# A graph network's first layer: own rows and input added by two accumulating DMAs into the sums' buffers, own rows stored already leaky, and a ninth mask made among the sums

## The chip, the core and the metric

The kernel runs on one core of a Trainium2 chip. The core has TensorE (PE, matmuls and transposes), VectorE (DVE), ScalarE (ACT), GpSimd (POOL) and SyncE (SP); each runs its own list of instructions in order, and waits on semaphores. DMAs are issued from the lists of SP, ScalarE and GpSimd. The metric is the device time of one execution in microseconds (us), lower is better.

## What is computed

A graph of 2708 nodes with 512 features, an adjacency matrix `adj` of integers (2708 x 2708, about 64 edges a row), and four layers, each followed by a residual and a layer norm. The change lies in layer 0; it also moves work of layer 1 that is prepared beside it:

```python
def L0(X, A, W_nb, b_nb, W_line, b_line):            # neighbours: the first 64 of each row
    Ab = A > 0
    keep = Ab & (cumsum(Ab, axis=1) <= 64)
    cnt = keep.sum(axis=1, keepdims=True)
    nb_mean = keep @ X / maximum(cnt, 1)
    xj = leaky_relu(nb_mean @ W_nb.T + b_nb)
    xi = leaky_relu(X @ W_line.T + b_line)            # the "own rows"
    return xi + where(cnt > 0, xj, 0)

def L1(x, adj, W_self, b_self, W_nb, b_nb, W_comb, b_comb):   # all neighbours
    mask = adj > 0
    agg = mask @ x / maximum(mask.sum(1), 1)
    return relu(concat([x @ W_self + b_self, agg @ W_nb + b_nb]) @ W_comb + b_comb)

x1 = layernorm(x + L0(x, ...))
x2 = layernorm(x1 + L1(x1, ...))
# layers 2 and 3: graph attention with 8 heads, then 8 heads and one head and a two-layer perceptron
```

## The kernel before

The 2708 rows are cut into `NT` = 22 tiles of 128 (the last, `LAST` = 21, has 20 rows). Products are taken before the sums: y = x W_nb is made once, and the neighbours' mean is a sum over y. y is kept as a high part `yH` and a low part `yL`, so each sum has two matmuls a neighbour tile. The change touches the first three of these stages.

**Layer 0's projections (0 to 193 us).** For each tile t: x is fetched and transposed by TensorE (L139, copied by L141), y = x W_nb (L300), split by ScalarE (L272) and VectorE (L277), own rows u = x W_line + b_line (bias added on VectorE, L452), stored to `r0_dram` by a GpSimd DMA (L453). Between these, masks are made, one for each tile of rows: loaded from `adj` with a cast to bf16 (L312, GpSimd's DMA), passed through a steep sigmoid that counts (`count`, L317, ScalarE), and in `place` a running sum over the row (a scan, L324) and a multiplication (L327) on VectorE mark the neighbours beyond the 64th. A finished mask must be transposed into `maskT`: either by TensorE, 22 transposes of 128 x 128 (`turn_here`, L336) and four signs on ScalarE (L340), or by one transposing DMA on SP (`turn`, L345) and four signs (L350). `HERE` = 14 masks are made in this stage; `now` spreads them over the tiles, and the even ones up to 10 are turned by DMA. Instructions on TensorE are held in the written order by `pe`, others by `issue_after`.

**Layer 0's sums (193 to 455 us).** The tiles of rows go in six blocks (`cuts`: five of four tiles, one of two). For each block and each neighbour tile j, ScalarE makes `kT` from `maskT` (L471), and TensorE adds into one PSUM buffer for each tile of the block (L639): eight matmuls a neighbour tile in the blocks of four. At the end ScalarE copies each sum to an SBUF buffer u, scaled by one over the count (L620). Beside the sums two generators are stepped by hand, and a scheduler puts their instructions into each engine's order:

- `both`, one step for each j: first `other_masks` (the remaining eight masks, 12 steps each: two half counts, four quarters of `place` of 677 columns, turn by DMA, signs at the next mask's steps), then `weights1` (W_nb and W_self of layer 1 multiplied into W_comb: rows fetched by SP, L205, transposed, L139, products, L300, a copy), then `vectors` (24 steps: a weight and an attention vector of layers 2 and 3 loaded by SP, L599 and L600, multiplied, L608, and reduced, L609).
- `todo`, two steps for each three j: `finish` of the block before. For each tile: bias (L530), leaky (L229), own rows fetched by SP (L205) into a `rows` buffer and made leaky (L229), x added onto them by an accumulating DMA (L534, GpSimd), combined with u (L536), layer norm (L121 to L128, its power on GpSimd, L126), x1 stored (L538), and its 32-bit words split into two halves of 16 bits (L149) and stored (L150) as `x1_words`.

**Layer 1's projections (455 to 612 us).** x1's transpose comes from `x1_words`: a transposing DMA on SP (L155) into a `rows` buffer (three of these), two tiles ahead, and a join on ScalarE (L161). Two products follow for each tile (L300): with the fused W_nb (split as before) and with the fused W_self (z, L667, stored by L669). The steps of `both` that are left (vectors) and of `todo` (the last block) come one a tile. Then layer 1's sums (612 to 830), and layers 2 and 3, which the change does not touch.

Of the kernel before, what the change touches and what calls it, by code (L numbers as in the profile page):

```python
# [10 lines left out]
F32 = mybir.dt.float32  # L11
# [9 lines left out]
P = 128  # L21
D = 512
# [10 lines left out]
def kernel(  # L33
# [18 lines left out]
    def rows(t):  # L52
        return min(P, N - t * P)
# [183 lines left out]
    with ExitStack() as phase:  # L237
# [65 lines left out]

        HERE = NT - 8
        cuts = [(b, min(b + 4, NT)) for b in range(0, NT, 4)]
        turns = range(NT)

# [47 lines left out]
        with ExitStack() as ph:  # L357
# [65 lines left out]
            for t in range(NT):  # L423
                n = rows(t)
                if t == END:
                    assert not due and turned >= HERE - 2
                    ends[:] = [end_tile(F32R) for _ in range(2)]
                    for y in (yH, yL):
                        nc.gpsimd.memset(y(LAST).bitcast(F32), 0.0)
                if t > 1:  # L430

                    lows[t] = keep_y(t, n, product(xTs(t, order=pe), n, wnT, 0, pe, sums() if t % 2 else None))
                xT = xTs(t)
                if t + 1 < NT:
                    xTs(t + 1, order=pe)
                while due and due[0][0] <= t:
                    signs_of(due.pop(0)[1], t)
                while turned < min(HERE, counted - (t + 2 < NT and not by_dma(turned))):
                    turn_next(turned)
                    turned += 1  # L440
                now = counted < min(HERE, -(-t * HERE // (NT - 4)))
                if now:
                    with tc.issue_after(stored[t - 1].ins) if t > 2 else nullcontext():
                        m = masks(counted)
                    places = st.tile([P, N // 2], BF16, name="places", bufs=1)
                    with tc.issue_after(highs[t].ins), tc.issue_after(copied[0].ins):
# [5 lines left out]
                low = nc.vector.tensor_add(u[:n], pm[:n], b_line[:n])  # L452
# [10 lines left out]
        with ExitStack() as ph:  # L463
# [10 lines left out]
            def other_masks():  # L474

                def room(i):
                    r = (ahead.tile([P, 2 * KD * (D + 2 * H)], BF16, name="w", tag="w", bufs=1) if i % 2 else
                         st.tile([P, 2 * KD * D], BF16, name="spare", tag="spare"))
                    m = r[:, :NT * P]
                    nc.gpsimd.memset(m[:, N if i < LAST else 0:], 0.0)  # L480
                    load_mask(i, m)
                    return m, r[:, NT * P:NT * P + N // 4 + 1]

                got, left = {HERE: room(HERE)}, iter(())
                into = weight2.rearrange("p k c -> p (k c)").bitcast(BF16)[:, :NT * P].rearrange("p (t n) -> p t n", n=P)
                for _ in range(5):
                    yield
                for i in range(HERE, NT):
                    if i + 1 < NT:
# [8 lines left out]
                    yield  # L498
                    for part in range(4):
                        place(i, m, places, part, 4)  # L500
                        if part == 3:
                            next(left, None)
                        yield
# [5 lines left out]
                    turn(i, m, into)  # L509
                    left = chain(signs(i, into), map(twins, turns[i:i + 1], [turns[i] + 1]))  # L510
                    yield
                    if i < LAST:
                        yield
                        yield
                signs_left.append(left)
                nc.vector.tensor_scalar(iso, cnts, 0.5, None, op0=OP.is_lt)
                nc.vector.tensor_scalar(rdeg, cnts, 1.0, None, op0=OP.max)
# [6 lines left out]
                nc.vector.reciprocal(one, one)  # L524

            def finish(ts_, us):
                r0s = early(1, len(ts_), lambda i: fetched(r0_dram, ts_[i], rows(ts_[i])))
                for i, t in enumerate(ts_):
                    n, u, r0 = rows(t), us[t], r0s(i)
                    nc.vector.tensor_add(u[:n], u[:n], b_nb[:n])  # L530
                    leaky(u[:n], u[:n])
                    with tc.issue_after(low.ins):
                        leaky(r0, r0)
                    nc.gpsimd.dma_start(r0, x[t * P:t * P + n, :], accum_op=OP.add)  # L534
                    yield
                    nc.vector.scalar_tensor_tensor(u[:n], u[:n], has[:n, t:t + 1], r0, op0=OP.mult, op1=OP.add)  # L536
                    layer_norm(sm, u[:n], n, u[:n])
                    nc.gpsimd.dma_start(x1_dram[t * P:t * P + n, :], u[:n])  # L538
                    yield
                    store_words(r0 if t % 2 or ts_ == range(*cuts[-1]) else words, x1_words, t, u)  # L540
                    yield


# [3 lines left out]
            bias1 = sm.tile([P, D], F32, name="bias1", bufs=1)  # L547

            def weights1():
                first, second = st.tile([P, KD, D], F32, name="spare", tag="spare"), weight2  # L550
                bcs = []
                order = [(w, m) for w in (l1_w_nb, l1_w_self) for m in range(KD)]
                load_weight(first, l1_w_comb[D:2 * D, :], nc.sync)
                nxt_rows = fetched(*order.pop(0), P)
                nc.sync.dma_start(bias1, bcast(l1_b_comb, D))
                for b_in in (l1_b_nb, l1_b_self):
                    bcs.append(sm.tile([P, KD], F32, name="bc"))
# [1 line left out]
                        nc.sync.dma_start(bcs[-1], b_in.rearrange("(k p) -> p k", p=P))  # L559
                yield  # L560
                for i, (bc, wc) in enumerate(zip(bcs, (first, second))):
                    dst = weight() if i == 0 else st.tile([P, KD, D], F32, name="spare", tag="spare")
# [59 lines left out]
            for i, b in enumerate(cuts):  # L622
                ts_ = range(*b)
                pa = {t: banks[t % 6]() for t in ts_}
                for j in range(NT):
                    if not kTs:
# [3 lines left out]
                            nxt, nxt_made = kept(b, following)  # L630
                        elif i + 1 < len(cuts):
                            nxt, nxt_made = kept(cuts[i + 1], 0)
                        with tc.issue_after(nxt_made.ins):
                            while copies:
                                copy_of(*copies.pop(0))
                    kT = kTs.pop(0)
                    for t in ts_:
                        for y in halves(j):
                            nc.tensor.matmul(pa[t], kT[:, (t - b[0]) * P:(t - b[0] + 1) * P], y(j),  # L639
                                             start=(j == 0 and y is yH), stop=(j == LAST))  # L640
                    if j % 3:
                        next(todo, None)
                    if len(ts_) > 2 or j % 2:
# [1020 lines left out]
```

## Time and profile before

| | |
|---|---|
| median of three runs | 2872.26 us (2871.07 to 2873.84) |
| the profiled execution | 2874.96 us |
| its span in the profile | 2873.2 us |
| granted TensorE clock, mean | 0.996 |
| layer 0's projections | 0 to 193 us |
| layer 0's sums | 193 to 455 us |
| layer 1's projections | 455 to 612 us |
| layer 1's sums | 612 to 830 us |

The profile has one execution on the core: a span from the first to the last instruction, busy time by engine, and groups of instructions by line of the kernel with what released them when they had waited. "PE acc L336 <- DVE u L452: 3.6" reads: a matmul of line 336 into the tile `acc` waited 3.6 us, and what ended the wait was VectorE's instruction of line 452 that writes `u`. Lines such as L300, L139, L205 and L229 are in helpers and stand for several places.

A few lines that give the durations of the work that the change moves (columns: line, engine, operation, output <- input, count, busy us, mean ns of one, idle time before and its releaser). First layer 0's projections:

```profile
L324 DVE TENSOR_TENSOR_SCAN places<-m,places,over 128x1354 bf16<-128x1354 bf16 x14 | 42.5, 3036 | 0.3
L327 DVE TENSOR_TENSOR m<-m,places 128x1354 bf16<-128x1354 bf16 x28 | 24.0, 859 | 0.4
L336 PE MATMUL acc<-identb,m 128*128 128x128 bf16 (+1 forms) x176 | 12.2, 220 | 3.6 <-DVE u L452 3.6
```

Then the sums and the start of layer 1's projections (193 to 480 us):

```profile
L530 DVE TENSOR_TENSOR u<-u,bias 128x512 f32<-128x512 f32 (+1 forms) x22 | 14.5, 672 | 5.4 <-ACT u L620 5.4
L229 DVE SCALAR_TENSOR_TENSOR rows<-rows 128x512 f32<-128x512 f32 x21 | 14.1, 684 | 29.0 <-DMA rows<-r_dram 29.0
L536 DVE SCALAR_TENSOR_TENSOR u<-u,has,rows 128x512 f32<-128x512 f32 x21 | 15.5, 745 | 21.1 <-DMA rows<-in_x_dram 21.1
```

### The profile page before, as it was taken

The numbers are of one execution on the slowest core, as the hardware profiler recorded it, in microseconds if no ns is written. First come the engines' busy times: TensorE is split into PE (matmuls) and PEld (weight loads), VectorE is DVE, ScalarE is ACT, GpSimd is POOL, SyncE is SP. The second block draws the span as 40 slices with busy tenths as digits, with TensorE's granted clock in tenths as the row PEclk, the third lists the DMA queues.
The fourth block names the chain that finished last, engine by engine and source line by source line (L and its number), as shares of the span: only waits on it lengthen the run. The fifth ranks groups of instructions, "written<-read, shape, count | busy, mean of one in ns | idle before, by whom it ended". The sixth has DMA issues, their size and how long they took to land. (4 is left out here: it accounts for less than half of the span.)

```text
span 2873.2 us, 35718 instructions
## 1 busy us (share of the span) xinstructions
PE 2801.1 (97%) x13910; PEld 1556.9 (54%) x13910; DVE 1992.8 (69%) x2372; ACT 1525.4 (53%) x1754; POOL 294.1 (10%) x457
## 2 busy tenths in 40 slices
PE   9999999999999999999999999999999999999998
PEld 5458764458886434444466433444385555555565
DVE  6856755643336999999978999999954435445342
ACT  4646642232336999999956999999950000000011
POOL 1112421111110000000021000000300010100001
PEclk9999999999999999999999999999999999999999
DMA  7745657533323011111152110111161000000000
GB/s 181 151 105 124 148 145 172 123 96 122 107 82 69 27 38 38 42 48 42 36 175 84 41 41 36 56 36 35 35 173 52 4 26 15 26 15 16 15 19 25
DMA packets 203654, 202.64 MB, mean 71 GB/s; under 512 B 126823, under 2 KB 151724, under 8 KB 203476
## 3 DMA queue, kind: packets, MB, share of 16 engines
q1 hardware_dynamic: 167592, 122.05, 16.2%
q0 software_dynamic: 24880, 74.01, 9.5%
q10 hardware_dynamic: 11004, 4.22, 0.6%
q8 instruction: 111, 1.82, 0.3%
q14 instruction: 67, 0.55, 0.1%
HBM read 137.90 MB, written 55.66 MB: 67 GB/s over the span
## 5 line engine op out<-in xcount | busy, mean ns | idle before, releaser
L894 DVE SCALAR_TENSOR_TENSOR e<-v_bc,ucol,maskT 128x1408 f32<-128x1408 f32 (+3 forms) x798 | 1133.0, 1483 | 315.5 <-PE pn L1295 307.3
L923 ACT ACTIVATE c<-e,bcol 128x1300 fp8e4<-128x1300 f32 (+2 forms) x688 | 956.7, 1412 | 61.7 <-DVE e L894 16.8
L1095 PE MATMUL po<-e,R 128*64 128x512 f32 (+3 forms) x4224 | 893.9, 549 | 25.8 <-DVE e L894 23.6
L1095 PEld LDWEIGHTS po<-e,R 128*64 128x64 f32 (+1 forms) x4224 | 333.7, 136 | 553.0 <-issue 390.0
L1295 PE MATMUL pn<-e,R 128*128 128x512 f32 (+1 forms) x1008 | 396.4, 557 | 0.8
L1295 PEld LDWEIGHTS pn<-e,R 128*128 128x128 f32 x1008 | 177.8, 190 | 195.5 <-issue 181.2
L1224 ACT ACTIVATE w<-pl,b 128x256 f32<-128x256 f32 (+1 forms) x88 | 40.9, 465 | 365.7 <-PE pl L1222 365.7
L126 POOL TENSOR_TENSOR ln_rs<-ln_rs,half 128x1 f32<-128x1 f32 (+1 forms) x88 | 56.7, 644 | 1321.6 <-DVE ln_rs L125 1300.4
L815 PE MATMUL pm<-w,xT 128*128 128x264 f32 (+1 forms) x704 | 164.1, 388 | 3.4 <-ACT xT L141 1.3
L686 PE MATMUL acc<-yH,mf 128*128 128x512 f32 x418 | 162.9, 390 | 0.0
L686 PE MATMUL acc<-yL,mf 128*128 128x512 f32 x418 | 162.8, 390 | 0.0
L1222 PE MATMUL pl<-lin 128*128 128x256 f32 (+1 forms) x704 | 152.9, 372 | 0.6 <-DVE lin L1124 0.6
L1247 PE MATMUL pl<-lin,w 128*128 128x512 f32 x336 | 150.8, 593 | 0.0
L1222 PEld LDWEIGHTS pl<-lin 128*128 128x128 f32 x704 | 129.5, 190 | 31.0 <-issue 15.8
L815 PEld LDWEIGHTS pm<-w,xT 128*128 128x128 f32 (+1 forms) x704 | 129.9, 190 | 28.9 <-ACT xT L141 3.5
L683 ACT CAST mf<-maskT 128x1024 fp32r<-128x1024 fp8e4 (+1 forms) x66 | 64.5, 978 | 142.9 <-PE acc L686 140.1
L995 PE MATMUL pd<-c,parts_c 128*12 128x384 fp8e4 (+2 forms) x2688 | 128.4, 307 | 0.0
L471 ACT ACTIVATE kT<-maskT 128x512 fp32r<-128x512 fp8e4 x121 | 75.9, 629 | 97.5 <-PE acc L639 80.3
L639 PE MATMUL acc<-yH,kT 128*128 128x512 f32 x304 | 123.0, 404 | 3.8 <-ACT kT L471 2.9
L300 PE MATMUL acc<-w,xT 128*128 128x512 f32 (+1 forms) x256 | 117.3, 602 | 5.1 <-ACT xT L161 2.7
L639 PE MATMUL acc<-yL,kT 128*128 128x512 f32 x304 | 119.9, 394 | 0.0
L1313 ACT COPY lin<-pn 128x512 f32<-128x512 f32 (+1 forms) x12 | 5.8, 538 | 204.6 <-PE pn L1295 204.6
(291 smaller groups left out, 3007.9 us busy)
## 6 DMA issues: line engine op xcount, KB each, us to landing
v_bc<-v_dram SPq DMA_DIRECT2D x16, 704.0 KB
x_dram<-u POOLq DMA_DIRECT2D x42, 256.0 KB, 2.4
v_bc<-v_dram SPq DMA_DIRECT2D x16, 650.0 KB
m<-in_adj_dram POOLq DMA_DIRECT2D x14, 677.0 KB, 7.1
rows<-in_x_dram SPq DMA_DIRECT2D x21, 256.0 KB
r_dram<-u POOLq DMA_DIRECT2D x21, 256.0 KB, 3.5
rows<-r_dram SPq DMA_DIRECT2D x21, 256.0 KB
rows<-in_x_dram POOLq DMA_DIRECT2D x21, 256.0 KB, 4.8
```

The costliest lines, as they stand in the source:

```text
L300: order(nc.tensor.matmul(pm[:m], xT[:, k, :m], w[:, k, :], start=(k == 0), stop=(k == KD - 1)))
L471: made = nc.scalar.activation(kT, maskT[:, j:j + g, b[0] * P:b[0] * P + w], AF.Relu, scale=-1.0)
L639: nc.tensor.matmul(pa[t], kT[:, (t - b[0]) * P:(t - b[0] + 1) * P], y(j), start=(j == 0 and y is yH), stop=(j == LAST))
L686: nc.tensor.matmul(pa, mf[:, j - g0, :], y(j), start=(j == 0 and y is yH), stop=(j == LAST))
L815: nc.tensor.matmul(pm[a][:m, :D // 2 + heads], xT[:, k, :m], w[:, k, a, :D // 2 + heads], start=(k == 0), stop=(k == KD - 1))
L894: self.made = nc.vector.scalar_tensor_tensor(e[:, :w], v[:, :w], ucol[:, j, h:h + 1], maskT[:, j, c0:c0 + w], op0=OP.max, op1=OP.mult)
L923: nc.scalar.activation(c[:, :w], e[:, :w], AF.Sigmoid, bias=bcol[:, j, h:h + 1], scale=STEP, saturate=False)
L995: pe(nc.tensor.matmul(p[32 * g:32 * g + 12, :c1 - c0], parts_c[:, j, h, :], c[:, c0:c1], start=(i == 0 and h == hs[0]), stop=(i == NT - 1 ...
L1095: pe(nc.tensor.matmul(po[i][HO * k:HO * k + HO, :c1 - c0], R2[at, j, h * HO:(h + 1) * HO], e[at, a:a + c1 - c0], start=(i_ == 0), stop=(i_ ...
L1222: nc.tensor.matmul(pl[:, :w], self.lin1[:, k, f * P:(f + 1) * P], h[:, k, :w], start=(k == 0), stop=(k == KD - 1))
L1247: nc.tensor.matmul(pl[:n], gT[:, f, (t - t0) * P:(t - t0) * P + n], self.lin2[:, f, :], start=(f == 0), stop=(f == KF - 1))
L1295: nc.tensor.matmul(pn[k][:, :w], R2[at, j, k * P:(k + 1) * P], e[at, :w], start=(j == 0), stop=(j == NT - 1))
```

## The change

- **Own rows are stored leaky.** In layer 0's projections a leaky on VectorE follows the bias add, before the store to `r0_dram`.
- **Two accumulating DMAs.** `finish` puts the bias on in one instruction (b_nb where the row has a neighbour, plus u), makes u leaky, and adds x and then the own rows from `r0_dram` into u by two accumulating DMAs on GpSimd's queue. This first step is taken for all tiles of the block, then layer norm, store and words for each. The fetch of own rows, their leaky and the combining instruction are gone; words of odd tiles and of the last block's tiles go into new `rows` buffers.
- **Nine masks among the sums.** `HERE` is 13, so eight masks become nine there, with ten steps for each instead of twelve, and a first wait of three steps instead of five.
- **Weight rows one ahead.** `weights1` fetches its rows one step before they are used, and its loading step is taken within the last mask's steps; the two large buffers `w` and `spare` swap roles.
- **Copies of the last two sums of a block** are made one a neighbour tile, at j = 1 and 2 of the next block, instead of both at once.

```diff
-        HERE = NT - 8
+        HERE = NT - 9
...
-                low = nc.vector.tensor_add(u[:n], pm[:n], b_line[:n])
+                nc.vector.tensor_add(u[:n], pm[:n], b_line[:n])
+                low = leaky(u[:n], u[:n])
                 stored[t] = nc.gpsimd.dma_start(r0_dram[t * P:t * P + n, :], u[:n])
...
-                for _ in range(5):
+                for _ in range(3):
                     yield
...
                         place(i, m, places, part, 4)
+                        if part == 0 and i == LAST:
+                            next(made_weights)
...
                     left = chain(signs(i, into), map(twins, turns[i:i + 1], [turns[i] + 1]))
                     yield
-                    if i < LAST:
-                        yield
-                        yield
...
             def finish(ts_, us):
-                r0s = early(1, len(ts_), lambda i: fetched(r0_dram, ts_[i], rows(ts_[i])))
-                for i, t in enumerate(ts_):
-                    n, u, r0 = rows(t), us[t], r0s(i)
-                    nc.vector.tensor_add(u[:n], u[:n], b_nb[:n])
+                for t in ts_:
+                    n, u = rows(t), us[t]
+                    nc.vector.scalar_tensor_tensor(u[:n], b_nb[:n], has[:n, t:t + 1], u[:n], op0=OP.mult, op1=OP.add)
                     leaky(u[:n], u[:n])
-                    with tc.issue_after(low.ins):
-                        leaky(r0, r0)
-                    nc.gpsimd.dma_start(r0, x[t * P:t * P + n, :], accum_op=OP.add)
+                    for src in (x, r0_dram):
+                        nc.gpsimd.dma_start(u[:n], src[t * P:t * P + n, :], accum_op=OP.add)
                     yield
-                    nc.vector.scalar_tensor_tensor(u[:n], u[:n], has[:n, t:t + 1], r0, op0=OP.mult, op1=OP.add)
+                for t in ts_:
+                    n, u = rows(t), us[t]
                     layer_norm(sm, u[:n], n, u[:n])
                     nc.gpsimd.dma_start(x1_dram[t * P:t * P + n, :], u[:n])
                     yield
-                    store_words(r0 if t % 2 or ts_ == range(*cuts[-1]) else words, x1_words, t, u)
+                    if t < LAST:
+                        even = t % 2 == 0 and t < cuts[-1][0]
+                        store_words(words if even else ahead.tile([P, D], F32, name="rows", bufs=3), x1_words, t, u)
                     yield
...
-                order = [(w, m) for w in (l1_w_nb, l1_w_self) for m in range(KD)]
+                w_rows = early(1, 2 * KD, lambda i: fetched((l1_w_nb, l1_w_self)[i // KD], i % KD, P))
                 load_weight(first, l1_w_comb[D:2 * D, :], nc.sync)
-                nxt_rows = fetched(*order.pop(0), P)
+                w_rows(0)
...
-                        xT = transposed(ahead, ps_tr, nxt_rows, P, "xT")
-                        nxt_rows = fetched(*order.pop(0), P) if order else None
+                        xT = transposed(ahead, ps_tr, w_rows(i * KD + m), P, "xT")
...
-            todo, both = iter(()), chain(other_masks(), weights1(), vectors())
+            made_weights = weights1()
+            todo, both = iter(()), chain(other_masks(), made_weights, vectors())
...
-                        with tc.issue_after(nxt_made.ins):
-                            while copies:
-                                copy_of(*copies.pop(0))
...
+                    if copies and j:
+                        with tc.issue_after(nxt_made.ins):
+                            copy_of(*copies.pop(0))
```

More of the change, by code (lines that the diff above doesn't have):

```diff
@@ L476, in room @@
                 def room(i):
-                    r = (ahead.tile([P, 2 * KD * (D + 2 * H)], BF16, name="w", tag="w", bufs=1) if i % 2 else
+                    r = (ahead.tile([P, 2 * KD * (D + 2 * H)], BF16, name="w", tag="w", bufs=1) if (i - HERE) % 2 else
                          st.tile([P, 2 * KD * D], BF16, name="spare", tag="spare"))
@@ L549, in weights1 @@
             def weights1():
-                first, second = st.tile([P, KD, D], F32, name="spare", tag="spare"), weight2
+                first, second = weight(), weight2
                 bcs = []
-                order = [(w, m) for w in (l1_w_nb, l1_w_self) for m in range(KD)]
+                w_rows = early(1, 2 * KD, lambda i: fetched((l1_w_nb, l1_w_self)[i // KD], i % KD, P))
                 load_weight(first, l1_w_comb[D:2 * D, :], nc.sync)
-                nxt_rows = fetched(*order.pop(0), P)
+                w_rows(0)
                 nc.sync.dma_start(bias1, bcast(l1_b_comb, D))
@@ L561, in weights1 @@
                 for i, (bc, wc) in enumerate(zip(bcs, (first, second))):
-                    dst = weight() if i == 0 else st.tile([P, KD, D], F32, name="spare", tag="spare")
+                    dst = weight() if i else st.tile([P, KD, D], F32, name="spare", tag="spare")
                     made1.append(dst)
```

## The prediction

> **What bounds the kernel now.** I read the busy totals first, then the same totals stage by stage (the stretches are layer 0's projections to 193 us, its sums to 455, layer 1's projections to 612, its sums to 830, the rest), then what ended TensorE's idle time in each.
>
> ```profile
> PE 2801.1 (97%) x13910; PEld 1556.9 (54%) x13910; DVE 1992.8 (69%) x2372; ACT 1525.4 (53%) x1754; POOL 294.1 (10%) x457
> ```
> ```profile
> 0.00:193.00 193.00, 185.31 (x666) 93.32 (x666) 141.02 (x128) 100.50 (x133) 32.30 (x64) 0.99 0.70 153
> 193.00:455.00 262.00, 252.69 (x1043) 194.35 (x1043) 164.94 (x278) 137.54 (x222) 75.51 (x102) 0.99 0.62 139
> 455.00:612.00 157.00, 150.89 (x359) 64.65 (x357) 93.77 (x124) 37.41 (x47) 19.06 (x31) 0.99 0.50 118
> ```
> The columns are stretch, its length, then busy time of PE, PE loads, VectorE, ScalarE, GpSimd. TensorE is busy 96% of each stretch, so VectorE, ScalarE and DMA work that goes away is worth nothing by itself: VectorE has 52, 97 and 63 us to spare. Only TensorE's own instructions and its waits can move the end. The diff touches nothing behind 612 us. The waits of TensorE, by stretch:
>
> ```profile
> PE acc L336 <- DVE u L452: 3.6, 1, 3.6
> PE acc L370 <- DVE ones L69: 1.1, 1, 1.1
> PE acc L300 <- DVE weight L178: 0.9, 1, 0.9
> PE acc L300 <- ACT maskT L340: 0.7, 1, 0.7
> ```
> ```profile
> PE ps_tr L139 <- DMA rows<-in_L_gnn_W_nb_dram: 4.3, 1, 4.3
> PE acc L639 <- ACT kT L471: 2.9, 1, 2.9
> PE acc L639 <- ACT u L620: 0.8, 1, 0.8
> PE ps_tr L139 <- DMA rows<-in_L_gnn_W_self_dram: 0.7, 1, 0.7
> ```
> ```profile
> PE acc L300 <- ACT xT L161: 2.7, 1, 2.7
> PE acc L300 <- DVE ln_rs L125: 1.6, 1, 1.6
> ```
> (waiting line, releaser, us in total, times, longest). Some 17 us in all, and the change can only win there and in removed matmuls. A long wait costs more than itself:
>
> ```profile
> 85.83 1.06 PE L336 MATMUL acc<-identb,m 128*128 128x128 bf16 x16
> 90.45 0.59 PE L336 MATMUL acc<-identb,m 128*128 128x128 bf16 x6 [3.55 <-DVE u L452]
> 90.97 5.40 PE L300 MATMUL pm<-weight,xT 128*128 128x512 f32 x8
> ```
> The eight products after the 3.55 us wait take 5.40 us where eight take 3.60 elsewhere in this stretch: 1.80 us more. The trace shows the same after the waits of 2.70, 2.93 and 4.34 us, not after 1.58.
>
> **A, layer 0's projections.** A turn by TensorE (22 transposes, L336) goes, since 13 masks instead of 14 are made here: 0.91 us for 16 plus 0.52 for 6 in the timeline, -1.43. The 3.55 us wait goes: it is mask 5's turn at tile 9, which needs a PSUM buffer freed by tile 8's bias add, and that add stood behind a 2.97 us scan on VectorE (86.84 to 89.73). In the new order this turn comes at tile 10, a tile after that add. -3.55 and -1.80. The 0.70 wait for L340, at another turn whose place moves, -0.70. Added: 21 leaky (L229, 0.68 us, one each 0.60) on VectorE, which also sheds two scans of 1354 (2 x 3.0) and two multiplications (2 x 0.86). VectorE's cycle of a tile with a mask grows from 8.87 to 9.47 us, so mask 1's second multiplication, which ends at 46.7 as TensorE gets to its turn, ends two leakys later: +1.3. At tile 15's turn the third group of transposes needs tile 14's add, again behind a scan: about 1.65 of the 3 us of that scan are left, +1.65. **A = -4.5** (-8 if neither new wait comes; up to +4 if two waits of 3.5 with their slow matmuls do: 13 x 7.7 + 18 x 2.03 = 137 us of VectorE stand in 141 us of TensorE there).
>
> **B, the sums.** Own rows come as an accumulating DMA into u (L532) instead of a fetch on SP, a leaky, an accumulate and an add: VectorE sheds 0.68 + 0.68 us for each of 22 tiles, worth nothing alone. A second accumulate waits for the first to land; one lands 4.73 us after its issue (median of L534, 3.09 to 9.15), so a tile is 2 x 4.7 us late where it was one. All four tiles are started before the first layer norm, and 14 calls of the block's list stand for 12 steps, so the block's 40 us hide it. Gone: the 2.93 us wait for kT at 319.22, behind a u copy (L620) that waited 1.86 us for the store of the old u, with 1.6 us of slow matmuls, and the 0.79 at 313.08 (copies now come one per neighbour tile, a block later than the store); the 4.34 at 385.03 with 1.3 slow and the 0.69 at 439.73 (weight rows are fetched one ahead). Sum -11.65. Added: ScalarE does two copies (0.69), two half counts (1.41) and kT (0.63) at a block's start, +1.3. On SP the transpose of mask 20 now stands behind a W_nb row fetch, whose buffer is free only when words of tile 11 have landed, some 38.4 us into block 3; behind the transpose (5.5 us at the shortest here) stand the signs of mask 20 on ScalarE's queue, then kT: a gap of 2.1 and 0.4 slow. The second W_comb load stands behind a W_self row fetch that waits for tile 13's words: +0.7. Signs of mask 21 +0.3. A ninth mask here takes the steps that each of the others gave up (10 instead of 12), 2.1 us of scan and multiplication a step. **B = -6.9** (-12 with no new wait, +4 if the queue's wait is as long as the transposed mask's own landing, 7.3, and comes twice).
>
> On this rests a rule that speaks against the change. The Trainium skill, "DMA: Bandwidth & Descriptors", section "Rules for kernel authors", says that an accumulating DMA beside another access of the same bytes can lose data and must wait for the earlier one's semaphore. The instruction order has just that wait on GpSimd's queue ahead of every second accumulate. By the rule alone the end of each block's rows is a landing later, which is what part C prices.
>
> **C, from the last block of sums to layer 1's projections.** Before, the first two transposed tiles xT (L161) were made at 441.9 and 446.2, before the sums ended at 455. In the new order SP issues the transposes of x_words behind the attention vectors' loads (L600): the load for step 7 waits for VectorE's reduce (L609) of step 5, which stands on VectorE behind tile 19's layer norm, which waits for its second accumulate. Worked from the start of the last block: tile 16's x is issued at 1.8, lands 6.5, its own rows 11.2; the others alternate on GpSimd's queue, tile 17's at 8.3, tile 18's at 12.1, then a store of x1, tile 19's at 14.9, landing 19.6. Twelve VectorE instructions follow to L609 of step 5 (eight at 0.6, four small, one wait of 0.75 for GpSimd's power): 25.5. The transpose lands some 3.7 later (3.5 to 4 here), 29.3, and ScalarE's join takes 1.17: 30.5. The sums end at 86 x 0.2285 = 19.7. TensorE waits 10.8, and 2.1 of slow matmuls: +12.9. The waits that stood here go: 1.58, 2.70 with 1.9 slow, two of 0.8 together: -7.0. **C = +5.9**. If VectorE's order didn't bind, tile 15's words and two u copies would still leave 5: -2; with none, -7; what it takes upwards is rival 3.
>
> The rule beside these rows is in the Trainium skill, "TensorE: Matmul & The Clock Gate", Part 1: half clock after about one idle window of 3.4 us, full clock after about as long busy. This trace has slow matmuls after a wait of 2.70 already, so the row decides; by the rule, as an estimate from that page, a wait of 10.8 costs at most half of 3.4, 1.7, in slow matmuls instead of 2.1, and the sum would be 0.4 lower.
>
> **Sum.** -4.5 - 6.9 + 5.9 = -5.5. The profiled execution took 2874.96 (span 2873.2), so 2869.5; the median of the three runs, 2872.26, is 2.7 below the profiled one, so **2866.7**.
>
> **Rivals.** (1) The wait in C is small: VectorE does its ready reduces without waiting for tile 19. For: VectorE is busy 60% there. Against: its instructions run in program order. C = -2 to -5, sum -13 to -16: about 2857. (2) New waits in B eat its gain: SP's queue carries mask transposes behind fetches that wait for words; in the trace SP already waits 83.7 us for words to land. B = -2 to +1, sum -1 to +2: about 2873. (3) Slower: in layer 1's projections SP's queue alternates transpose and vector load, and a load waits for VectorE's pair of the step two before. If nothing of that overlaps, a tile's round is a vector step (2.7 to 3.4), the transpose's landing (3.5 to 4) and the join (1.17): 7.4 to 8.6, against TensorE's 2 x 3.44 = 6.9 for a tile. Over some ten tiles that is +5 to +17 on top of C. It decides from 1.2 us a tile on, where the sum -5.5 + 12 passes +5.7; from there to 1.7 it is +6 to +11: about 2880. For: every transpose but two has a load ahead of it. Against: three buffers of rows let transposes run ahead, and the sum of parts that overlap is less. (4) The diff doesn't do what it says: no sign; the order has 22 more accumulates and 22 fewer fetches of own rows.
>
> **Chances.** Forecast (-2 to -10, 2862 to 2870) 0.42; (1) 0.22; (2) 0.20; (3) 0.16. A difference of 0.2%, 5.7 us, is about what a measurement of this kernel can tell from no change: half of the forecast's own case lies below -5.7 (0.22) and half above. Faster 0.22 + 0.22 = 0.44; same 0.20 + 0.20 = 0.40; slower 0.16. The range leaves out the best fifth of (1) and the upper two thirds of (3), together some 0.15: 2856 to 2879.
>
> **What would show it.** A: no wait of L336 for L452 at tile 9, 154 transposes L336 instead of 176, waits of 1 to 2 us at tiles 4 and 15. B: no wait for W_nb rows, none for the u copy, one of about 2 us for kT early in block 4. C: a wait of 7 to 12 us of the first L300 of layer 1 for xT, ended by a transpose. Wrong if that wait is under 5 (then rival 1), if waits for kT in the sums come to over 8 (rival 2), or if more than two waits over 2 us stand behind the first in layer 1's projections (rival 3).

## The result and the profile after

The changed kernel takes 2918.25 us (median of six, 2909.96 to 2922.66) where the kernel before takes 2875.25 beside it (2871.07 to 2878.51): ratio 1.0146, 95% interval 1.0127 to 1.0165. The profiled execution took 2910.97, span 2909.1; before it was 2874.96 and 2873.2. So the kernel is slower, by 36 us in the profiles and 43 in the medians, where -5.5 was forecast. The profiled execution is one of the two fastest of the six, so the last 7 us of the medians stand in no trace; what follows explains the 36.

The totals of the page, then the first three of the four stretches (length, then busy time of PE, PE loads, VectorE, ScalarE and GpSimd, granted clock, DMA share, GB/s), cut at the changed kernel's own borders: first matmul of the sums, last one, first matmul of layer 1's sums. In the kernel before these lie at 188.8, 455.0 and 613.5; the prediction's view of it was cut at 193, 455 and 612.

```profile
PE 2802.9 (96%) x13888; PEld 1556.4 (54%) x13888; DVE 1984.4 (68%) x2355; ACT 1525.8 (52%) x1756; POOL 306.5 (11%) x480
```
```profile
0.00:193.30 193.30, 180.54 (x634) 90.54 (x634) 145.47 (x144) 94.08 (x125) 30.26 (x58) 0.98 0.63 144
193.30:473.70 280.40, 259.60 (x1053) 196.81 (x1052) 150.75 (x240) 141.78 (x229) 82.74 (x120) 0.97 0.67 131
473.70:645.10 171.40, 151.47 (x361) 65.54 (x360) 96.77 (x131) 42.18 (x51) 26.34 (x42) 0.95 0.53 127
```

TensorE does the same work (2802.9 against 2801.1 us, 22 transposes fewer), so the 36 us are nearly all waits, and matmuls at the lower clock after them. Measured between the same events, before and after: projections 188.8 and 193.3, sums 266.2 and 280.4, layer 1's projections 158.5 and 171.4, the rest 2259.7 and 2264.0. That is +4.5, +14.2, +12.9 and +4.3. VectorE, which the change relieves, has lost 8 us of work, and the kernel is slower all the same. TensorE's waits in the three stretches, in this order:

```profile
PE acc L300 <- ACT maskT L340: 5.3, 1, 5.3
PE acc L336 <- DVE u L452: 3.1, 1, 3.1
```
```profile
PE pm L637 <- ACT kT L472: 11.5, 3, 7.9
PE ps_tr L300 <- issue: 3.5, 1, 3.5
PE pm L637 <- ACT u L621: 3.1, 1, 3.1
PE acc L637 <- ACT kT L472: 2.3, 3, 1.0
```
```profile
PE acc L300 <- ACT xT L161: 17.7, 1, 17.7
```

The waits that the change was expected to end are gone: none for W_nb rows, none at 90 us, none behind a u copy at 319. Others, longer, stand in their place.

**The 17.7 us wait** is the forecast one of part C. Three views of it, by time: GpSimd's DMA issues, VectorE, and SP's queue, from the last block of sums on (block start 453.8, its sums' end 473.7).

```profile
468.77 0.84 POOL L532 DMA_DIRECT2D u<-r_dram  x1 [3.91 <-DMA u<-in_x_dram]
...
472.11 0.89 POOL L532 DMA_DIRECT2D u<-r_dram  x1
```
```profile
478.07 0.69 DVE L121 BATCH_NORM_STATS2 ln_st<-u 128x6 f32<-128x512 f32 x1 [3.47 <-DMA u<-r_dram]
...
483.53 0.68 DVE L609 TENSOR_REDUCE wa<-weight 128x8 f32<-128x512 f32 x1
```
```profile
474.47 10.13 SPq L600 DMA_DIRECT2D weight<-in_L_gnn_W_dram  x3
484.65 3.87 SPq L155 DMA_TRANSPOSE rows<-x_words  x2
```

Own rows of tile 19 are issued at 472.11 and land at 478.0; the reduce behind that layer norm ends at 484.2; only then SP's third load of the three in the view goes, and behind it, at 484.65, the first transpose of x_words. ScalarE's join waits for it until 490.36, and TensorE's first product of layer 1 starts at 491.57. The accumulates' medians from issue to landing, in us (last column), where the kernel before had 4.73:

```profile
u<-in_x_dram POOLq DMA_DIRECT2D x21, 256.0 KB, 6.4
u<-r_dram POOLq DMA_DIRECT2D x21, 256.0 KB, 5.0
```

**The 7.9 us wait** in the sums, at 380.73, is the one that was forecast with 2.1. SP again, then ScalarE:

```profile
362.64 10.43 SPq L205 DMA_DIRECT2D rows<-in_L_gnn_W_nb_dram  x2
373.23 3.89 SPq L345 DMA_TRANSPOSE weight<-w  x1
```
```profile
379.10 1.06 ACT L350 ACTIVATE maskT<-weight 128x1024 fp8e4<-128x1024 bf16 x1 [8.56 <-DMA weight<-w]
380.06 0.61 ACT L472 ACTIVATE kT<-maskT 128x512 fp32r<-128x512 fp8e4 x1
```

The second fetch of a weight row stands 10 us for words of tile 11 to land; the transpose of mask 20 is behind it; its signs head ScalarE's queue for 8.56 us, and kT, for which TensorE waits, stands behind the signs.

**Three more waits in the sums.** The next longest for kT, 3.4 us at 273.32, has the same form, but no fetch of a weight row is ahead of its transpose. The transpose itself is slow, and so is an accumulate issued beside it, which landed at 268.49. GpSimd, SP and ScalarE:

```profile
256.71 0.85 POOL L532 DMA_DIRECT2D u<-r_dram  x1 [0.46 <-DMA u<-in_x_dram]
```
```profile
256.73 7.04 SPq L345 DMA_TRANSPOSE weight<-spare  x1
```
```profile
271.69 1.06 ACT L350 ACTIVATE maskT<-weight 128x1024 fp8e4<-128x1024 bf16 x1 [4.64 <-DMA weight<-spare]
```

The wait of 3.1 us for a u copy, at 285.7, stands behind a half count on ScalarE that waited 2.2 us for its mask's load. The one of 3.5 us, for which the profile names no releaser, is put down here to W_comb's second load: it ends at 426.25, and VectorE's first instruction on the same tile, at 426.18, was released by that load:

```profile
L575 DVE SCALAR_TENSOR_TENSOR u<-weight,bc,u 128x512 f32<-128x512 f32 x4 | 3.0, 752 | 11.9 <-DMA weight<-in_L_gnn_W_comb_dram 11.8
```

**The 5.3 us wait** in the projections, at 104.08, was not forecast:

```profile
91.92 0.54 POOL L454 DMA_DIRECT2D r_dram<-u  x1 [5.06 <-DVE u L229]
...
92.58 0.73 POOL L312 DMA_DIRECT2D m<-in_adj_dram  x1
```
```profile
100.47 2.55 ACT L317 ACTIVATE m<-m,gate 128x2708 bf16<-128x2708 bf16 x1 [6.01 <-DMA m<-in_adj_dram]
...
103.02 2.64 ACT L340 ACTIVATE maskT<-acc 128x1024 fp8e4<-128x1024 bf16 x4
```

The store of own rows waits on GpSimd's queue for the new leaky; the next mask's load is behind the store and lands 7.8 us later; the count waits for it; and the signs of the turn before, which free TensorE's PSUM buffers, are behind the count.

### The profile page after: what moved, and what is told of

Read it like the earlier page. It is cut to its first block, busy times and chain, and to the rows that moved or that the text cites. A ratio compares the mean times of both kernels' runs of the same rounds, so it can differ in the third digit from the quotient of the medians.

```text
span 2909.1 us, 35610 instructions
## 1 busy us (share of the span) xinstructions
PE 2802.9 (96%) x13888; PEld 1556.4 (54%) x13888; DVE 1984.4 (68%) x2355; ACT 1525.8 (52%) x1756; POOL 306.5 (11%) x480
## 3 DMA queue, kind: packets, MB, share of 16 engines
q0 software_dynamic: 27984, 79.55, 10.6%
```

## The experiments

Ratios are to the kernel before, run on the same chip. The stage times are of each profiled execution, between the events named above; "start wait" is TensorE's longest wait ahead of layer 1's first products. Kernels whose code is the same in a stage differ there by up to 4 us (seven kernels have the changed kernel's first stage: 191.5 to 195.4).

| kernel | ratio (95%) | projections | sums | layer 1's projections | start wait |
|---|---|---|---|---|---|
| before | 1 | 188.8 | 266.2 | 158.5 | none |
| changed | 1.0146 (1.0127 to 1.0165) | 193.3 | 280.4 | 171.4 | 17.7 |
| b_finish | 1.0061 (1.0044 to 1.0078) | 190.3 | 276.5 | 156.9 | none |
| b_nine | 0.9991 (0.9981 to 1.0000) | 185.6 | 269.0 | 155.5 | none |
| b_rows | 0.9995 (0.9986 to 1.0005) | 189.4 | 264.3 | 159.2 | none |
| b_copies | 1.0010 (1.0000 to 1.0020) | 190.3 | 268.4 | 158.2 | none |
| a_old_finish | 1.0018 (1.0009 to 1.0028) | 185.3 | 272.3 | 158.3 | 3.2 |
| b_finish_nine | 1.0091 (1.0074 to 1.0108) | 195.2 | 276.1 | 166.7 | 13.7 |
| a_vec_late | 1.0120 (1.0103 to 1.0137) | 191.5 | 277.1 | 171.0 | 17.0 |
| a_step_late | 1.0116 (1.0099 to 1.0133) | 195.4 | 277.1 | 168.0 | 14.4 |
| a_no_x | 1.0008 (0.9998 to 1.0017) | 191.8 | 259.5 | 161.3 | 7.6 |
| a_no_leaky | 1.0138 (1.0121 to 1.0155) | 186.4 | 283.2 | 171.5 | 17.2 |
| a_front | 1.0082 (1.0065 to 1.0098) | 191.5 | 276.8 | 157.5 | none |
| a_sum_store | 1.0041 (1.0026 to 1.0056) | 212.1 | 259.5 | 160.4 | 5.9 |
| a_per_tile | 1.0116 (1.0100 to 1.0133) | 194.7 | 282.4 | 172.4 | 13.2 |
| c_gp_add | 1.0073 (1.0051 to 1.0095) | 216.1 | 256.7 | 151.2 | none |
| c_nine_fetch | 1.0055 (1.0037 to 1.0073) | 221.2 | 260.2 | 151.2 | none |
| c_eight_fetch | 1.0032 (1.0019 to 1.0045) | 215.7 | 255.1 | 150.5 | none |
| d_eight_early_x | 0.9999 (0.9991 to 1.0008) | 202.4 | 255.2 | 151.9 | none |
| d_nine_early_x | 0.9992 (0.9983 to 1.0001) | 199.1 | 258.6 | 151.2 | none |

### The parts alone

Each is a part of the change's own diff on the kernel before. **b_finish** has the leaky at the store and the new `finish`:

```diff
+                low = leaky(u[:n], u[:n])
...
+                    for src in (x, r0_dram):
+                        nc.gpsimd.dma_start(u[:n], src[t * P:t * P + n, :], accum_op=OP.add)
```

> The kernel before with the new finish alone: own rows stored leaky, two accumulating DMAs into u, words of odd tiles in new buffers; masks, weight rows, copies as before. Queue theory (the loss of 36 us is short instructions standing in an in-order queue behind DMA landings that the change made later, above all SP's transposes of x_words behind vector loads that start earlier): the vectors start where they did, so only a landing of 5 us comes on top at the last block: +3 to +10 us. DMA theory (42 accumulates of 256 KB beside mask loads and transposes make every DMA slower): +15 to +25 us, most of it in the sums. Mask theory (the ninth mask overfills the sums): within 4 us of before.

+0.61%, some 17 us: the DMA theory's range, and over half of it (10.3 us) in the sums. Layer 1's start has no long wait. In the projections, with 14 masks as before, the leaky shows 1.5 us, less than kernels with the same code differ by.

**b_nine** has the ninth mask, the shorter steps, and `w` and `spare` swapped:

```diff
+        HERE = NT - 9
...
-                    if i < LAST:
-                        yield
-                        yield
```

> The kernel before with nine masks among the sums in ten steps each (13 in the projections), w and spare swapped; finish, weight rows and copies as before. Queue theory: the vectors start at the last block's start, as in the changed kernel, and the transposes of x_words stand behind their loads, with one accumulate less ahead: a wait of 5 to 10 us at layer 1's start, the sums some 3 us worse by the crowding of the masks, 1.4 us won by one turn less: +5 to +15 us. DMA theory: 0 to +5. Mask theory: +20 to +30, most of it in the sums.

-0.09%. The queue theory's +5 to +15 and the mask theory's +20 are both out; the DMA theory's 0 to +5 is nearest. The vectors start as early here as in the changed kernel, 4 to 5 us ahead of the last block, and with one accumulate less there is no long wait behind them.

**b_rows** and **b_copies**:

```diff
+                w_rows = early(1, 2 * KD, lambda i: fetched((l1_w_nb, l1_w_self)[i // KD], i % KD, P))
```
```diff
+                    if copies and j:
+                        with tc.issue_after(nxt_made.ins):
+                            copy_of(*copies.pop(0))
```

> The kernel before with the weight rows fetched one ahead, nothing else. All theories: the 4.34 us wait for W_nb rows with 1.3 us of slow matmuls and the 0.69 for W_self rows go: -4 to -6. If the early fetch stands behind words that have not landed, it only moves: 0.

> The kernel before with the copies of a block's last two sums made one a neighbour tile at j = 1 and 2, nothing else. All theories: the 2.93 us wait for kT at 319 us with 1.6 us of slow matmuls and part of the 0.79 us go: -3 to -5.

Neither is a gain that the measurement tells from none. In b_rows the wait for W_nb rows is 3.04 us instead of 4.34, and the one for W_self rows 0.54 instead of 0.69. In b_copies the stall behind the u copy is ended (the copy waits 0.18 us for its store instead of 1.86), but another comes, of 4.11 at 328.5: kT behind the signs of a mask, which wait 5.38 us for its transpose. Part B had counted both stalls as gone.

**a_old_finish**: the changed kernel with the `finish` and the store of before, so b_finish's lines taken back:

```diff
-                low = leaky(u[:n], u[:n])
...
+                    nc.gpsimd.dma_start(r0, x[t * P:t * P + n, :], accum_op=OP.add)
```

> The changed kernel with the finish of before (own rows fetched, made leaky there, one accumulate) and own rows stored as before; nine masks, weight rows and copies as changed. By parts alone (+17, -3, -0.5, +3) the finish is the only dear part, but the parts come to +17 and the whole to +42. Theory 1, interaction: the finish is dear because the nine masks put vectors, counts and transposes into the steps where its landings fall, so without it the rest is near before: -4 to +3. Theory 2, the nine masks are dear with the other small parts: +15 to +25.

+0.18%, some 5 us (interval 2.6 to 8.0): without the new finish the change is near before. Theory 2 falls; theory 1 is near, with its -4 to +3 a little low.

**b_finish_nine**: the two diffs of b_finish and b_nine together.

> The kernel before with the new finish and the nine masks; weight rows and copies as before. Theory 1: the interaction is between these two, +35 to +42, with the long wait for x_words at layer 1's start and the long waits in the projections. Theory 2: they add, +14.

+0.91%, where the two alone add to +0.52%. The interaction is there, though not all of the +1.46%: by the stages alone one would add up to 187.1, 279.3 and 153.9; together they have 195.2, 276.1 and 166.7, so 8 us in the projections and 13 at layer 1's start come from the two meeting. The changed kernel adds weight rows one ahead and the copies, which were worth nothing alone, and with them come 4.3 us more in the sums and 4.7 more at layer 1's start of the profiles, and 0.55% in the ratios; which of the two does it was not tried.

### The queue in front of layer 1, and the mask transpose

**a_vec_late** and **a_step_late**:

```diff
             def vectors():
+                for _ in range(11):
+                    yield
```
```diff
-                        if part == 0 and i == LAST:
-                            next(made_weights)
```

> The changed kernel, with eleven empty steps before the attention vectors, so that their loads come behind the first transposes of x_words on SP and no vector stands in VectorE's queue in the last block. Queue theory: the 17.7 us wait at layer 1's start falls to about the chain of landings itself (tile 16's words need the copy, two landings, layer norm, a store and a transpose), to 4 to 8 us: -10 to -14. Rival: the wait is set by the accumulates and the u copies, and stays over 14: -4 to 0.

> The changed kernel without the early loading step of the weights, so that SP's transpose of mask 20 no longer stands behind the fetch of a weight row that waits for words of tile 11. Queue theory: the 7.88 us wait for kT with some 1.2 us of slow matmuls goes, and a wait of up to 6 for W_comb or weight rows takes its place: -3 to -9. Rival: the signs wait for the transpose's own landing, and the wait stays: within 3 us of the changed kernel.

Neither did what it was made for. The waits stay (17.0, and 7.5 for kT), but in a_vec_late's trace several vector loads still stand ahead of the first transpose on SP, and in a_step_late's the weight rows' fetch still stands ahead of mask 20's transpose: the scheduler orders SP's queue, and the edits did not change this. They do not refute the queue. But a_vec_late shows that it is not the whole wait: its first transpose is issued 5 us after the sums' end instead of 11, and ScalarE's join waits for it until 10.6 us after that issue, where it was 5.7 in the changed kernel, so the wait hardly shrinks.

**a_front** does it by a dependency, on top of a_vec_late's empty steps:

```diff
+                    with tc.issue_after(turned_last[0].ins):
                         nc.sync.dma_start(*w_view(wr, w_src, k))
...
-                        even = t % 2 == 0 and t < cuts[-1][0]
+                        even = t < cuts[-1][0] and (t % 2 == 0 or t >= cuts[-2][0])
```

> The changed kernel with the first transposes of x_words ahead of the vector loads on SP, and words of tiles 16 to 19 all in one buffer, so that these transposes wait for no landing of words. If SP's queue and the shared buffers set the wait at layer 1's start, 17.7 us falls to under 4: -14 to -20. Rival: ScalarE's queue sets it, where xT stands behind the copy of tile 21's sum, which waits for the store of x1 of tile 17: the wait stays at 7 to 10, -7 to -11.

The start wait is gone, layer 1's projections are 157.5, 13.9 us less than the changed kernel's, and the rival (ScalarE's u copies) is out; a wait of 4.4 us for yL comes behind the start. SP's queue in it:

```profile
441.96 3.04 SPq L157 DMA_TRANSPOSE rows<-x_words  x2
445.10 0.53 SPq L604 DMA_DIRECT2D weight<-in_L_gnn_a_dram  x1
```

The first transposes are issued 26 us before its sums end (468.3), where the changed kernel issues them 11 us after. The edit changes order and buffer together; which of the two would have been enough was not tried.

### The second accumulate

**a_no_x** leaves x out of the result:

```diff
-                    for src in (x, r0_dram):
+                    for src in (r0_dram,):
```

> The changed kernel with one accumulating DMA a tile instead of two: x is left out of the residual. Landing theory (what costs is that u is ready a landing of 5 to 8 us later, and words, x1's stores, the u buffers and the transposes of x_words follow from it): the 17.7 us wait falls below 9 and the sums lose 3 to 8 us: -12 to -20 against the changed kernel. Rival (vectors and masks crowd the queues whatever the accumulates do): -5 to 0.

The sums fall to 259.5, 20.9 us below the changed kernel and 6.7 below the one before; the start wait falls to 7.6. In all its profile is 37 us below the changed kernel's, about twice what the landing theory allowed (12 to 20). The waits in the sums:

```profile
PE acc L637 <- ACT kT L472: 2.7, 1, 2.7
PE pm L637 <- ACT kT L472: 0.8, 2, 0.6
```

Mask 20's transpose is behind the same fetch on SP here, but is issued 165 us after the sums' start instead of 180, as tile 11's words land sooner. So the queue was the place, and the second accumulate the cause: its landing, its traffic, or both, since the edit takes away both.

**a_per_tile** finishes each tile before the next:

```diff
                     for src in (x, r0_dram):
                         nc.gpsimd.dma_start(u[:n], src[t * P:t * P + n, :], accum_op=OP.add)
                     yield
-                for t in ts_:
-                    n, u = rows(t), us[t]
```

> The changed kernel with the old order within finish: bias, leaky, two accumulates, layer norm, store and words of one tile before the next tile's, instead of the first step for all four. If the two accumulates in a row cost wherever they stand: the sums stay at 277 to 283 us, within 6 us of the changed kernel. If it is the batch of four (four tiles' landings ahead of the first layer norm): the sums fall towards 266, -8 to -15.

Sums 282.4: the batch of four is not the cause; two accumulates in a row cost as much in either order.

**a_no_leaky** leaves the leaky of own rows out of the result:

```diff
-                low = leaky(u[:n], u[:n])
```

> The changed kernel with own rows stored as they are, the leaky left out altogether. If the leaky makes the projections slower (a store on GpSimd's queue waits for it, the next mask's load stands behind the store, the count waits for the load): the first sums start at 185 to 187 us instead of 193, -6 to -9. Rival: the mask loads are late for another reason, and it is worth its own VectorE time alone: -2 to 0.

Projections 186.4, 6.9 us less (5 less than the fastest with the changed kernel's code there), and the wait for L340 is 1.5 instead of 5.3. With 14 masks, in b_finish, the leaky brought no wait for L340, so the price belongs to leaky and 13 masks together. As a whole the kernel is no faster than the changed one beyond the intervals: the sums are 283.2.

### Taking the accumulate out of the sums

**a_sum_store**: in the projections, one tile behind the store, and one accumulate in `finish`:

```diff
+                    nc.gpsimd.dma_start(r0_dram[a:z, :], x[a:z, :], accum_op=OP.add, max_dma_last_dim=D)
```

> The changed kernel with x added to the stored own rows already in the projections, by an accumulating DMA in DRAM one tile behind the store, so that finish has one accumulate. Landing theory: the sums and layer 1's start gain what the kernel without x gains (-12 to -20), less what 22 more DMAs on GpSimd's queue cost the mask loads in the projections (0 to +8). Rival: the projections lose more than that, +10 and over.

Sums 259.5, as without x, though the result is whole: 21 us are won there and 11 at layer 1's start. The projections lose 19 us against the changed kernel, as the rival had it, one wait of 17.3 for L340 among it. In sum +0.41% over before.

**c_gp_add**, **c_nine_fetch**, **c_eight_fetch**: x is added by GpSimd before the store; the first with one accumulate in `finish` and a_front's edits, the others on the kernel before, without any accumulate (its leaky and its L534 dropped), with nine and with eight masks.

```diff
+                nc.gpsimd.tensor_add(u[:n], u[:n], xs(t)[:n])
                 stored[t] = nc.gpsimd.dma_start(r0_dram[t * P:t * P + n, :], u[:n])
```

> The changed kernel with x added to the leaky own rows by GpSimd (an add of 128x512) before the store, one accumulate in finish, and the first transposes of x_words ahead of the vectors with words of tiles 16 to 19 in one buffer. Landing theory: sums 259 to 262 us as with x left out, layer 1's projections 156 to 158 as with the transposes in front, so below the kernel before if the add on GpSimd's queue holds the mask loads up by less than 8 us: -8 to +2 against before. Rival: the queue holds them up as the accumulate in DRAM did (+19 us in the projections): +8 to +15.

> The kernel before with nine masks among the sums, own rows stored leaky and with x added by GpSimd, and in finish the fetch of before without its leaky and without any accumulate. A landing less than before in each tile: sums 262 to 267, no wait for weight rows behind own rows longer than before; projections 190 to 196 by leaky and add: -4 to +6 against before. If own rows' readiness was never what set the sums of before, nothing is won there: +4 to +8.

> The same with eight masks among the sums as before: the projections hold 14 masks, and leaky and add cost +1 to +6 there (leaky alone cost 1.5 with 14 masks); sums 262 to 267: -4 to +6 against before.

The sums fall to 255 to 260 and layer 1's projections to 151, more than expected. All of it and more is paid in the projections, 216 to 221 us, and all three kernels are slower than their forecasts and rivals allowed. The way is another than forecast. TensorE's longest waits in c_eight_fetch's projections:

```profile
PE ps_tr L139 <- DMA rows<-in_x_dram: 15.1, 8, 4.7
PE acc L300 <- ACT maskT L340: 7.2, 2, 4.9
```

It waits for rows of x, whose three buffers are held until GpSimd's add has read them (1.3 us long in most tiles, 3.9 in seven).

**d_eight_early_x**, **d_nine_early_x**: the accumulate goes into u ahead of the store, and the store is issued one tile later.

```diff
+                stored[t] = nc.gpsimd.dma_start(u[:n], x[t * P:t * P + n, :], accum_op=OP.add)
+                if t:
+                    nc.gpsimd.dma_start(r0_dram[t * P - P:t * P, :], before_u)
+                before_u = u
```

> As c_eight_fetch (eight masks among the sums, own rows leaky and with x when stored, no accumulate in finish), but x is added in the projections by an accumulating DMA into u, and the store of a tile's rows is issued one tile later, so that nothing holds x's rows and GpSimd's queue waits for no landing. Landing theory: sums 255 to 260, layer 1's projections 150 to 152 as there, and projections 190 to 196 instead of 215.7: -8 to -20 against before. Rival: 22 accumulates beside the mask loads cost the projections as much again (over 205): 0 to +5.

> The same with nine masks among the sums in ten steps each. The nine masks alone were worth -2.6 us in the kernel before, but leaky with 13 masks cost 7 us in the projections: within 6 us of d_eight_early_x, rather above it.

Sums 255.2 and 258.6, layer 1's projections 151.9 and 151.2, so 18 and 15 us won behind the projections; and projections 202.4 and 199.1, 14 and 10 us lost, between the forecast's 190 to 196 and the rival's 205. Both lie within 0.2% of before: no version here beats it by more than the measurement tells. What takes the gain, in d_eight_early_x's projections:

```profile
PE acc L336 <- DVE u L452: 9.6, 3, 6.1
PE acc L336 <- DVE m L327: 3.3, 3, 1.7
```

The bias add L452 now waits for a u buffer until accumulate and store have landed, and the turns wait for it; a mask load takes 9.2 us (median) where it took 7.1 before.

## Why the prediction was wrong

The sign and the size were wrong. The mechanisms that it named were mostly right; their prices were not, and one queue was left out. Its own sign for rival 2, waits for kT of over 8 us in the sums, came with 13.8; but that rival too was priced far too low, at -1 to +2 in all.

- **A, forecast -4.5, measured +4.5.** Right: the wait at 90 us went, with the 1.43 us of a turn, and the two new waits came (0.83 at 47 us for 1.3; 3.08 at 144 us for 1.65). Wrong: the step "the 0.70 wait for L340, at another turn whose place moves, -0.70". In its place one of 5.34 came, at 104 us. The leaky was priced on VectorE alone. What is queued behind it is the store on GpSimd, then a mask's load, then a count, then the signs. a_no_leaky gives the leaky's price beside 13 masks: 6.9 us.
- **B, forecast -6.9, measured +14.2.** The failed step is "the block's 40 us hide it". It was read as a question whether each block's list ends in time. It does end, but the words of a tile are also what frees a buffer for a weight row, and SP's queue carries a mask's transpose behind that row. The place had been named and priced 2.1 us, from the words' landing by the durations of single accumulates; it cost 7.9. W_comb's load, priced 0.7, cost 3.45. The waits of 3.4 us behind a slow transpose and 3.1 for a u copy had no term at all. And of the stalls that were counted as gone, the one for W_nb rows only shrinks when its part is made alone, and the one behind the u copy gives way to another.
- **C, forecast +5.9, measured +12.9.** The chain was right link by link, and the terms that were mis-sized are the accumulate and the transpose. The accumulate was put at 4.73 us, the median of the kernel before with one a tile; the changed kernel's medians, from issue to landing, are 6.4 for x and 5.0 for own rows. Tile 19's own rows landed 24.3 us after the block's start instead of 19.6, and the transpose took 5.7 instead of 3.7: 4.7 + 2.0 are nearly all of the 6.9 by which 17.7 exceeds 10.8. Rival 3's alternating queue did not come: after the first wait layer 1's projections have no long one.
- **The rest, not forecast, +4.3.** 3.3 us of it lie behind the last store of the program (below). The other 1.0 is not explained; it is within what kernels with the same code there differ by.

The stage sums are 4.5 + 14.2 + 12.9 + 4.3 = 35.9. Of the change's parts, a_old_finish leaves the new finish with its leaky as the dear one (1.0146 against 1.0018), and a_no_x within it the second accumulate (1.0008). What stays open is how much of the second accumulate is its own wait and how much the slowing of other DMAs: taking it away takes both away. The trace has signs of the second: the mask's transpose at 256.73 landed by 271.69, 15.0 us after its issue, where the one at 373.23 took 5.9, and the accumulate issued with it took 11.8.

On the two rules weighed ahead: the wait that the Trainium skill's "DMA: Bandwidth & Descriptors", "Rules for kernel authors", requires between accumulates on the same bytes belongs to the dearest thing in the change. a_no_x measures that wait, the second accumulate's traffic and all that follows in one: 21 us in the sums and 10 at layer 1's start. In the skill's "TensorE: Matmul & The Clock Gate", Part 1, full clock comes back after at least one busy window of about 3.4 us, so the prediction's "at most" did not follow from it. Here the granted clock, by stretches of 2 us, was 0.50 until some 4.6 us after 491.57, and the eight matmuls there took 5.98 us instead of 3.60: 2.4 more, above the estimate of 1.7 and near the 2.1 of the sum.

## What to carry to other kernels

A landing that is added to a chain is to be followed to every buffer that the chain frees and to every queue that holds an instruction for such a buffer; an engine that waits there stops all that is queued behind, whatever its own load is. Take a DMA's duration from rows in which as many run beside it as will run after the change. And where a stall is to be ended, follow what is late next before it is counted: of the two that were tried alone here, one only shrank, and another, longer one came in place of the other. Where the second accumulate's work was moved out of the sums into the projections, the projections lost much of what was won, or more.

## What the runs showed that was not expected

The program's end took longer in kernels with more accumulating DMAs. After the last store GpSimd's queue drains; the columns are count and least, median and longest duration in ns. In order: the changed kernel (44 accumulates), the kernel before (22), c_eight_fetch (none):

```profile
L1660 POOLq DRAIN  x3: 46/107/6030, 2902.2 to 2908.8; - x3
```
```profile
L1659 POOLq DRAIN  x3: 46/107/3411, 2868.9 to 2872.9; - x3
```
```profile
L1658 POOLq DRAIN  x3: 46/107/1532, 2875.7 to 2878.2; - x3
```

All kernels with 44 have 6.03 to 6.07, those with 22 have 3.33 to 3.49, those with none 1.53. In a_sum_store, with 22 into SBUF and 22 into DRAM, it is 2.02, so it does not go by their number alone, and what sets it is not shown. The instruction before it, INC_SWDGE_SEM, goes the same way in the three kernels, 1.66, 1.02 and 0.55 us.
